# A planner's rule for PSUM banks at the attention visits, and a new order of all instructions

## The chip, the cores and the metric

The kernel runs on one core of a Trainium2 chip. The time is device microseconds of one execution; several runs give a median. The engines are PE (TensorE, matrix products), DVE (VectorE), ACT (ScalarE), POOL (GpSimd) and SP, whose queue issues nearly all DMAs.

## What is computed

The input is 64 graphs of 256 nodes with 512 features each, and one 256 x 256 adjacency that all of them share. Two attention layers follow each other, each with a layer norm and a ReLU in front and a residual behind. All is float32.

```python
h = jnp.maximum(_layernorm(x), 0.0)          # layer 0, one head, additive scores
Wh = h @ W
logits = (Wh @ a_src)[:, :, None] + (Wh @ a_dst)[:, None, :]
logits = jnp.where(logits >= 0, logits, 0.2 * logits)
attn = softmax(where(adj == 0, -inf, logits))
x = x + attn @ Wh

h = jnp.maximum(_layernorm(x), 0.0)          # layer 1, 8 heads of 64
q, k, v = split_heads(h @ Wq.T + bq), split_heads(h @ Wk.T + bk), split_heads(h @ Wv.T + bv)
attn = softmax(where(adj == 0, -inf, q @ k.T / 8))
x = x + (merge_heads(attn @ v)) @ Wo.T + bo
```

## The kernel before

**Graphs and pairs.** One graph is two tiles of 128 nodes. Graphs go in pairs, an even one g and an odd one g + 1, and 31 of the 32 pairs run the same stages. The names of the tiles tell the stages in the profile, since every instruction is issued from one line, 430.

**Stages of layer 0**, for each graph: `normalize0` (ACT computes mean and squares, then writes h), `weights0` (e1, e2 and em; their sums over the nodes go through PE as ps and prs; the row es_b is spread to all partitions by DMAs), `aggregate0` (PE products pu, which ACT copies into uT; POOL then forms the four sums us), and `transform0`, which multiplies by W and adds into x. In the profile that is po_a<-w_sb and po_b<-w_sb; in the programs' names po0.

**Stages of layer 1.** `normalize1` makes xn, and `transpose1` transposes it: DVE by blocks into z, then through DRAM (the DMAs rows and hT) into left. `project` makes q, k and v for a pair at once (the products pp, with weight sums that the DMAs wst bring in each time from `products` in DRAM). `attention` follows per graph, then `scale` and `output`, which multiplies by Wo (po_a<-wo_sb, po_b<-wo_sb; po1 in the programs' names) and stores.

**Products in series.** The projections and the two multiplications by W and Wo use Strassen's scheme with seven products instead of eight, the projections on two levels. `chained` runs seven products through two PSUM banks, a and b: a, b, a, b, a, b, a. After each product DVE (in some cases ACT) reads the bank and adds it into its target. Before the next product of the same bank may start, that read must be done. Such a series is a *chain*: it holds two banks from its first product to its last read. A block is what PE issues in one piece: four passes for po, six for pp.

**Attention and its visits.** `scores(e)` makes the scores of two heads, in two banks psc; four such steps (e = 0 to 3) fill eight banks, one after the other. ACT reads each bank with an exponential into ex. DVE multiplies ex by the mask (ex<-ex,pmask) and forms the sums sm. `values` makes pav from ex and v, which ACT copies into aT; `head_sums` makes psm, whose reciprocal rc goes by the DMAs row and rb to all partitions and scales aT. The planner joins the steps into three visits that PE runs in one piece: A is the scores of the even graph, B the values and head sums of the even graph with the scores of the odd one behind, C the values and head sums of the odd graph (`VISITS`, line 186).

**What sets the order.** All instructions are recorded first. `Plan.schedule` then simulates the engines with a cost for each instruction and writes an order for each of the five queues; on the chip every queue runs in that order, with semaphores. PE's blocks are sorted by a due place that `PHASE` gives to each stage (in units of graphs). At each point the planner takes the first block among the next `AHEAD` whose inputs are there and for which enough PSUM banks are open. Seven banks are shared out; the eighth keeps the mask. A block that opens a bank needs one, a block that opens a chain needs two, and the second one stays reserved (`reserved`) until the chain takes it. To enter a visit at least `ROOM` = 2 banks must be open besides the reserved ones; if they aren't, the planner goes on to later blocks. Inside a visit (`visit` is not empty) only its own blocks are taken. The engines' instructions are taken in the order of a latest time, which `SLACK` shifts. `SPARE`, `POOLED` and `LANDING` stretch the assumed times of DVE and ACT, of POOL and of DMAs.

The loop over PE's blocks is the place of the change:

```python
todo = [(blocks.index(visit[0]), visit[0])] if visit else enumerate(blocks[:ahead])
for n, block in todo:
    when = startable(block)
    ...
    if block.peers and not visit:
        need = max(need, ROOM)
    if len(open_banks) < need + others:
        continue
```

Of the kernel before, what the change touches and what calls it, by code (L numbers as in the profile page):

```python
# [144 lines left out]
class Op:  # L145
# [10 lines left out]


SIGNAL = 0.06
AHEAD = 24
SLACK = 4.95106  # L160
SPARE = 1.05024
STEPS = {"first": 6, "project": 49, "transform0": 7, "output": 7, "aggregate0": 3}
ASIDE = 0.9
PHASE = {
    "project0": [-0.11788, 0.21271, 0.48678, 1.00731, 1.0573, 1.46327, 1.80536, 2.01641],
    "aggregate00": [-1.17147, -0.98045],
    "aggregate01": [-0.53658, -0.25084],
    "output0": [2.37181, 2.56087, 2.64717],
    "output1": [3.26166, 3.33686, 3.61644],
    "transform00": [-1.01934, -0.99938, -0.77151],  # L170
    "transform01": [-0.48014, -0.39696, 0.06805],
    "weights00": [-1.85072],
    "weights01": [-0.68932],
    "A": [1.60905],
    "B": [2.0676],
    "C": [2.4008],
    "first0": [0.0443, 0.37448],
    "first1": [0.71863, 1.33943],
    "A0": [0.77194],
    "B0": [1.59602],  # L180
    "C0": [2.25334],
}
LANDING = 2.98188
POOLED = 1.1
ROOM = 2
VISITS = {(0, False): ("A", 0), (0, True): ("B", 0), (1, False): ("B", 10), (1, True): ("C", 0)}

# [1 line left out]
class Plan:  # L189
# [96 lines left out]
    def schedule(self, ahead, slack):  # L286
        self.deadlines(slack)
        left = {op.at: len(op.deps) for op in self.ops}
        ready = {e: [] for e in ("vector", "scalar", "gpsimd", "sync")}
        waiting = {e: [] for e in ready}  # L290
        free = dict.fromkeys((*ready, "tensor"), 0.0)
        times, now = [0.0], 0.0
        bank_free, reserved = [0.0] * (self.banks + 1), {}
        blocks, tile_kind, visit = list(self.blocks), None, []
        port = queue = 0.0

        def release(op):
            for o in op.next:
                left[o.at] -= 1
                if not left[o.at] and o.engine != "tensor":  # L300
                    known = max(ready_at(o, d) for d in o.deps.values())
                    heapq.heappush(waiting[o.engine], (known, o.at))
                    heapq.heappush(times, known)

        def ready_at(op, dep):
            if op.engine == dep.engine == "tensor":
                return dep.start + dep.step
            return dep.done + SIGNAL

        def finish(op, start):  # L310
            nonlocal port, queue
            spare = 1.0 if op.engine == "tensor" else POOLED if op.engine == "gpsimd" else SPARE
            op.start, op.done = start, start + op.time * spare
            end = start + op.step * spare
            if op.port:
                wait = max(0.0, port - start)
                op.done += wait
                port = max(port, start) + 0.05 if op.brief else op.done
                end += wait
            if op.transfer:  # L320
                queue = max(queue, start + 0.6 * LANDING) + op.transfer * SPARE
                op.done = queue + 0.4 * LANDING
            free[op.engine] = end
            heapq.heappush(times, end)
            release(op)
            for v in (*op.outs, *op.ins):
                base = v.base
                if base.bank is not None and all(o.done is not None for o in base.ops):
                    bank_free[base.bank] = max(o.done for o in base.ops) + SIGNAL
                    heapq.heappush(times, bank_free[base.bank])  # L330

        def startable(block):
            block = [op for b in block.peers for op in b] if block.peers and not visit else block
            inside = set(o.at for o in block)
            when = 0.0
            for op in block:
                for d in op.deps.values():
                    if d.at not in inside:
                        if d.done is None:
                            return None  # L340
                        when = max(when, ready_at(op, d))
            return when

        for op in self.ops:
            if not op.deps and op.engine != "tensor":
                heapq.heappush(waiting[op.engine], (0.0, op.at))
        total = len(self.ops)
        order = []
        while len(order) < total:
            assert times, [[o.outs[0].base.name for o in b][:1] for b in blocks[:4]]  # L350
            now = heapq.heappop(times)
            while times and times[0] <= now:
                heapq.heappop(times)
            for e in ready:
                while waiting[e] and waiting[e][0][0] <= now:
                    at = heapq.heappop(waiting[e])[1]
                    heapq.heappush(ready[e], (self.ops[at].late, at))
                if free[e] <= now and ready[e]:
                    op = self.ops[heapq.heappop(ready[e])[1]]
                    order.append(op)  # L360
                    finish(op, now)
            if free["tensor"] <= now:
                open_banks = [n for n, t in enumerate(bank_free[:-1]) if t <= now]
                todo = [(blocks.index(visit[0]), visit[0])] if visit else enumerate(blocks[:ahead])
                for n, block in todo:
                    when = startable(block)
                    if when is None or when > now:
                        if when is not None:
                            heapq.heappush(times, when)
                        continue  # L370
                    new = {
                        id(o.outs[0].base): o.outs[0].base
                        for o in block
                        if o.outs[0].base.bank is True
                    }
                    need, others = len(new), sum(reserved.values())
                    for base in new.values():
                        if base.chain is not None:
                            if base.chain in reserved:
                                others -= reserved[base.chain]  # L380
                            else:
                                need = 2
                    if block.peers and not visit:
                        need = max(need, ROOM)
                    if len(open_banks) < need + others:
                        continue
                    for base in new.values():
                        base.bank = min(open_banks, key=lambda b: bank_free[b])
                        open_banks.remove(base.bank)
                        bank_free[base.bank] = math.inf  # L390
                        if base.chain is not None:
                            reserved[base.chain] = reserved.get(base.chain, 2) - 1
                            if not reserved[base.chain]:
                                del reserved[base.chain]
                    t = now
                    late = now > free["tensor"] + 0.01
                    for op in block:
                        if op.kind != tile_kind:
                            t += 0.1 if tile_kind == (P, P) else 0.2
                            tile_kind, late = op.kind, True  # L400
                        finish(op, t)
                        t += op.step + (0.1 if late else 0.0)
                        late = False
                        order.append(op)
                    free["tensor"] = t
                    heapq.heappush(times, t)
                    del blocks[n]
                    if block.peers:
                        visit = (visit or block.peers)[1:]
                    break  # L410
        self.order = sorted(order, key=lambda op: ((op.block or [op])[0].start, op.at))
        return max(op.done for op in order)
# [97 lines left out]
def kernel(  # L510
# [1369 lines left out]
    with ExitStack() as ctx_b:  # L1880
# [5 lines left out]
        bounded(plan)  # L1886
        plan.schedule(AHEAD, SLACK)
        ps_mm = ctx_b.enter_context(tc.tile_pool(name="ps_mm", bufs=1, space=PSUM))
# [38 lines left out]
```

## Time and profile before

| | us |
|---|---|
| median of three runs | 2775.09 |
| lowest and highest | 2773.01, 2775.99 |
| the profiled execution | 2773.59 |
| its span, first to last instruction | 2771.7 |
| busy time of POOL, q1's share of the 16 DMA engines | 1195.3, 57.5% |
| ACT, exponentials ex<-psc, 512 of them | 259.8, mean 0.616 |
| DVE, masks ex<-ex,pmask, 512 of them | 317.0, mean 0.681 |
| DVE, sums sm<-ex, 256 of them | 167.4, mean 0.687 |
| wst<-products, 651 transfers of 384 KB, issue to landing | 4.6 |

A row of a group tells the engine, the operation, the tiles written and read, their shapes and the count; then the busy time in the whole run, the mean of one in nanoseconds, and the idle time before it with what ended that. A PE matmul's busy time reaches to its modelled end, some time after the next one has started, so a block's cost is read from its start to the start of the next block. A float32 product appears as two passes: 2048 rows of psc are 1024 matmuls.

In a timeline each row has the start, the length, the engine, the instruction and a count of neighbours that are merged.

### The profile page before, as it was taken

How to read it: one execution, taken by the hardware profiler on the slowest of the kernel's cores; microseconds unless marked ns; L12 is line 12 of the kernel's file. 1: busy time of each engine (PE TensorE's matmuls, PEld its weight loads, DVE VectorE, ACT ScalarE, POOL GpSimd, SP SyncE). 2: the span in 40 equal slices, each digit the busy share in tenths (PEclk: the TensorE clock that was granted, in tenths of full speed). 3: DMA queues.
4: the chain of work that ended last, by engine and by line, in shares of the span. 5: the costliest groups of instructions: out<-in, count | busy, mean ns of one | idle time of the engine just before them, and what ended most of it. 6: DMA issues, size and time to landing. Idle time of an engine off the chain costs nothing.

```text
span 2771.7 us, 60664 instructions
## 1 busy us (share of the span) xinstructions
PE 2733.5 (99%) x22588; PEld 2390.8 (86%) x22588; DVE 2224.5 (80%) x4879; ACT 1343.6 (48%) x3332; POOL 1195.3 (43%) x1153
## 2 busy tenths in 40 slices
PE   7999999999999999999999999999999999999998
PEld 5888888888888888888888888888898888888886
DVE  6677888888888888888788888888888888887876
ACT  5754454444554544544444545445545445444431
POOL 3344444444444444444444344444444444445431
PEclk9999999999999999999999999999999999999999
DMA  5455565565555655655655555565556656556662
GB/s 182 160 178 162 176 190 175 171 190 184 179 182 172 190 182 175 184 179 173 196 178 181 187 177 175 184 181 184 182 177 189 185 175 184 175 173 197 181 183 91
DMA packets 278926, 493.32 MB, mean 178 GB/s; under 512 B 45473, under 2 KB 150756, under 8 KB 278630
## 3 DMA queue, kind: packets, MB, share of 16 engines
q1 hardware_dynamic: 278534, 489.39, 57.5%
q8 instruction: 183, 3.00, 0.5%
q14 instruction: 113, 0.93, 0.1%
q0 software_dynamic: 96, 0.01, 0.0%
HBM read 405.09 MB, written 76.20 MB: 174 GB/s over the span
## 4 chain that ended last, share of the span: by engine, by line
PE 88%; DVE 3%; DMA 3%; ACT 3%; POOL 2%; issue 1%; SPq 0%; POOLq 0%; DVEq 0%
PE pp_a L430 20%; PE po_a L430 15%; PE pp_b L430 15%; PE po_b L430 11%; PE psc L430 9%; PE pu L430 8%; PE pav L430 4%; ACT xn L430 2%; PE psm L430 1%; DMA x<-in_x_dram 1%; POOL em L430 1%; PE pqk L430 1%; DMA out_dram<-x 1%; PE ps L430 1%; DVE nmr L430 1%; POOL rstd L430 1%
## 5 line engine op out<-in xcount | busy, mean ns | idle before, releaser
L430 POOL TENSOR_TENSOR c<-tt,c 128x768 f32<-128x768 f32 x124 | 232.6, 1896 | 402.8 <-DVE tt L430 305.8
L430 DVE TENSOR_TENSOR ex<-ex,pmask 128x512 f32<-128x512 f32 x512 | 317.0, 681 | 33.0 <-ACT ex L430 32.9
L430 PE MATMUL psc<-c 64*128 64x256 f32 x2048 | 292.1, 400 | 5.7 <-ACT aT L430 3.3
L430 DVE TENSOR_TENSOR x<-po_a,x 128x256 f32<-128x256 f32 x500 | 209.3, 419 | 107.9 <-PE po_a L430 105.3
L430 PEld LDWEIGHTS psc<-c 64*128 64x128 f32 x2048 | 205.6, 187 | 79.9 <-ACT ex L430 21.7
L430 ACT ACTIVATE ex<-psc 128x512 f32<-128x512 f32 x512 | 259.8, 616 | 28.9 <-PE psc L430 28.7
L430 POOL TENSOR_TENSOR us<-uT 128x256 f32<-128x256 f32 x126 | 107.8, 855 | 314.7 <-ACT uT L430 300.7
L430 PE MATMUL pu<-em,h 128*128 128x256 f32 x1008 | 239.0, 380 | 0.3 <-ACT c L430 0.3
L430 PE MATMUL pav<-ex,c 128*64 128x256 f32 x2048 | 235.1, 382 | 0.0
L430 ACT COPY uT<-pu 128x512 f32<-128x512 f32 x126 | 73.9, 586 | 322.4 <-PE pu L430 322.3
L430 DVE SCALAR_TENSOR_TENSOR junk<-wa,h 128x512 f32<-128x512 f32 x252 | 206.3, 819 | 21.9 <-ACT h L430 19.7
L430 PEld LDWEIGHTS pav<-ex,c 128*64 128x64 f32 x2048 | 141.4, 137 | 73.1 <-issue 0.9
L430 PEld LDWEIGHTS pu<-em,h 128*128 128x128 f32 x1008 | 184.9, 191 | 22.5 <-issue 0.7
L430 POOL TENSOR_TENSOR x<-x,bo_b 128x512 f32<-128x512 f32 x128 | 160.9, 1278 | 92.4 <-ACT xn L430 87.4
L430 ACT ACTIVATE e<-es_b,ed 128x256 f32<-128x256 f32 x122 | 61.1, 501 | 287.1 <-issue 158.0
L430 DVE TENSOR_TENSOR tt<-tt,pp_a 128x384 f32<-128x384 f32 x279 | 153.4, 550 | 50.9 <-PE pp_a L430 46.0
L430 POOL TENSOR_TENSOR as<-aT 128x256 f32<-128x256 f32 x62 | 67.3, 1085 | 286.4 <-DVE aT L430 277.9
L430 POOL TENSOR_TENSOR em<-e,maskT 128x512 f32<-128x512 f32 x62 | 78.9, 1273 | 257.4 <-DVE e L430 248.4
L430 DVE TENSOR_TENSOR c<-c,pp_a 128x384 f32<-128x384 f32 x217 | 119.2, 549 | 80.3 <-ACT xn L430 45.3
L430 DVE TENSOR_TENSOR x<-po_b,x 128x256 f32<-128x256 f32 x375 | 156.3, 417 | 31.2 <-PE po_b L430 27.4
L430 ACT ACTIVATE h<-x,nmr,rstd 128x512 f32<-128x512 f32 x128 | 100.4, 810 | 157.5 <-DVE nmr L430 153.3
L430 DVE TENSOR_TENSOR sm<-ex 128x512 f32<-128x512 f32 x256 | 167.4, 687 | 0.0
(274 smaller groups left out, 7510.6 us busy)
## 6 DMA issues: line engine op xcount, KB each, us to landing
wst<-products SPq DMA_DIRECT2D x651, 384.0 KB, 4.6
wst<-products SPq DMA_DIRECT2D x217, 192.0 KB, 4.4
x<-in_x_dram SPq DMA_DIRECT2D x64, 512.0 KB, 5.2
out_dram<-x SPq DMA_DIRECT2D x128, 256.0 KB, 2.3
rows<-z SPq DMA_DIRECT2D x62, 512.0 KB, 4.2
hT<-rows SPq DMA_DIRECT2D x248, 128.0 KB, 3.3
rb<-row SPq DMA_DIRECT2D x124, 256.0 KB, 4.2
products<-made SPq DMA_DIRECT2D x21, 384.0 KB, 2.8
```

Of the source, the lines that this page charges most:

```text
L430: getattr(getattr(self.nc, op.engine), op.method)(*map(real, op.args), **{k: real(a) for k, a in op.kwargs.items()})
```

## The change

In the planner's loop a flag is added. As soon as a visit has been met whose inputs are there, but which is not entered for lack of banks, no later block is taken that opens a bank, unless that bank is the second one of a chain which is already running. Blocks of running chains go on. The constants of the planner are new, and with them the order of all instructions and the numbers of the banks; the instructions themselves, the buffers and the DMAs stay as they are.

```diff
-AHEAD = 24
-SLACK = 4.95106
-SPARE = 1.05024
+AHEAD = 49
+SLACK = 8.77484
+SPARE = 1.01674
...
 PHASE = {
-    "project0": [-0.11788, 0.21271, 0.48678, 1.00731, 1.0573, 1.46327, 1.80536, 2.01641],
-    "aggregate00": [-1.17147, -0.98045],
-    "aggregate01": [-0.53658, -0.25084],
-    "output0": [2.37181, 2.56087, 2.64717],
-    "output1": [3.26166, 3.33686, 3.61644],
+    "project0": [-0.19438, 0.14752, 0.34467, 0.44171, 0.46305, 0.81839, 1.07542, 1.17863],
+    "aggregate00": [-1.53219, -1.41296],
+    "aggregate01": [-0.59454, -0.51794],
+    "output0": [2.23584, 2.29763, 2.36253],
+    "output1": [2.92165, 2.98377, 3.36758],
...
-    "A": [1.60905],
-    "B": [2.0676],
-    "C": [2.4008],
+    "A": [1.52703],
+    "B": [1.72599],
+    "C": [2.68772],
...
-LANDING = 2.98188
-POOLED = 1.1
+LANDING = 3.47999
+POOLED = 1.24146
...
                 todo = [(blocks.index(visit[0]), visit[0])] if visit else enumerate(blocks[:ahead])
+                draining = False
                 for n, block in todo:
...
                     if block.peers and not visit:
                         need = max(need, ROOM)
+                        draining = True
+                    elif draining and any(b.chain not in reserved for b in new.values()):
+                        continue
                     if len(open_banks) < need + others:
                         continue
```

Around the visits the order of one pair in the middle of the run changes thus. Before, A is followed by blocks of po1, po0 and pp in turn, and by B 24.0 us of PE work later (from scores to scores); after, A is followed by six blocks of po0, one pp, the seventh po0 and one more pp, and by B 15.7 us later. Before, the eight banks of A are 5, 7, 2, 3, 5, 7, 2, 3 and those of B's scores 5, 2, 4, 7, 3, 5, 2, 4; after, 2, 7, 0, 6, 1, 3, 5, 2 and 0, 7, 3, 5, 2, 0, 7, 3. On ACT the copy into aT stood between the writing of xn and the mean for the next h, with the exponentials of B behind all three; after, that copy stands ahead of xn, and the mean for h behind the exponentials.

More of the change, by code (lines that the diff above doesn't have):

```diff
@@ L164 @@
 PHASE = {
-    "project0": [-0.11788, 0.21271, 0.48678, 1.00731, 1.0573, 1.46327, 1.80536, 2.01641],
-    "aggregate00": [-1.17147, -0.98045],
-    "aggregate01": [-0.53658, -0.25084],
-    "output0": [2.37181, 2.56087, 2.64717],
-    "output1": [3.26166, 3.33686, 3.61644],
[L170 to L173, printed above, removed]
-    "A": [1.60905],
-    "B": [2.0676],
-    "C": [2.4008],
[L177 to L181, printed above, removed]
-}
-LANDING = 2.98188
-POOLED = 1.1
+    "project0": [-0.19438, 0.14752, 0.34467, 0.44171, 0.46305, 0.81839, 1.07542, 1.17863],
[3 more added lines that the diff above has]
+    "output1": [2.92165, 2.98377, 3.36758],
+    "transform00": [-1.77316, -1.33036, -1.07346],
+    "transform01": [-1.92842, -0.97066, -0.51583],
+    "weights00": [-1.72871],
+    "weights01": [-0.9223],
+    "A": [1.52703],
+    "B": [1.72599],
+    "C": [2.68772],
+    "first0": [0.80489, 0.83087],
+    "first1": [1.72404, 1.86629],
+    "A0": [0.70038],
+    "B0": [1.66422],
+    "C0": [2.86714],
+}
+LANDING = 3.47999
+POOLED = 1.24146
 ROOM = 2
```

## The prediction

> **What bounds the kernel now.** I read the page's first part, then the waits of PE, then its groups with shapes kept apart, then the timeline of one pair of graphs. The page says that PE is the bound and that its clock is granted in full.
>
> ```profile
> span 2771.7 us, 60664 instructions
> PE 2733.5 (99%) x22588; PEld 2390.8 (86%) x22588; DVE 2224.5 (80%) x4879; ACT 1343.6 (48%) x3332; POOL 1195.3 (43%) x1153
> PEclk9999999999999999999999999999999999999999
> ```
>
> 99% leaves 38 us of idle PE, and the list of its waits sums to 31 us, 25 of them in the first 300 us. So a gain has to come from inside the busy time. The groups show where:
>
> ```profile
> L430 PE MATMUL psc<-c 64*128 64x256 f32 x2048 | 292.1, 400 | 5.7 <-ACT aT L430 3.3
> ...
> L430 PE MATMUL pav<-ex,c 128*64 128x256 f32 x2048 | 235.1, 382 | 0.0
> ```
>
> psc (scores) and pav (values) have equal counts and 256 columns each, and both run two at a time on half of the array; the scores take 57 us more. The timeline shows it in every pair:
>
> ```profile
> 1386.89 4.41 PE L430 MATMUL psc<-c 64*128 64x256 f32 x32
> 1391.23 1.13 PE L430 MATMUL po_a<-wo_sb,aT 128*128 128x256 f32 x4
> ...
> 1411.68 4.85 PE L430 MATMUL psc<-c 64*128 64x256 f32 x32
> 1416.46 0.71 PE L430 MATMUL pp_a<-sa,wst 128*128 128x128 f32 x4
> ```
>
> From its start to the start of the next block, a visit to an even graph's scores takes 4.34 us, an odd graph's 4.78. Over the run 30 even visits take 4.34 and 28 odd ones 4.78. The next visit of the same kind begins 84.2 us later. Six visits are different, among them these:
>
> ```profile
> 126.04 3.72 PE L430 MATMUL psc<-c 64*128 64x256 f32 x32
> 129.69 1.13 PE L430 MATMUL pu<-em,h 128*128 128x256 f32 x4
> ...
> 202.01 3.92 PE L430 MATMUL psc<-c 64*128 64x256 f32 x32
> 205.86 0.71 PE L430 MATMUL pp_b<-sc,wst 128*128 128x128 f32 x4
> ```
>
> They take 3.65 and 3.85. The banks written into the programs explain them. A visit fills eight. Where the program gives it six or seven different ones (three visits) it takes 3.65. With five it takes 3.85 (202.01, and another at 2675.93) if ACT begins the exponentials at once. With four it takes 4.34: its fifth matmul waits for the first exponential. The odd ones have five banks as well, but take 4.78, because ACT comes late:
>
> ```profile
> 1411.28 1.52 ACT L430 ACTIVATE xn<-x,nmr,rstd 128x512 f32<-128x512 f32 x2 [1.52 <-DVE nmr L430]
> 1412.71 0.56 ACT L430 COPY aT<-pav 128x512 f32<-128x512 f32 x1
> 1413.17 0.63 ACT L430 ACTIVATE h<-x 128x512 f32<-128x512 f32 x1
> 1413.71 0.19 ACT L430 ACTIVATION_READ_ACCUMULATOR h<-x 128x1 f32 x1
> 1413.80 3.99 ACT L430 ACTIVATE ex<-psc 128x512 f32<-128x512 f32 x8
> ```
>
> In an even visit the first exponential starts 1.17 us after the visit (1388.06); here 2.12, so 0.95 late, and 3.85 + 0.95 is 4.80. Outside the visits PE runs from block to block: six passes of pp in 0.67, four of po in 0.865, with 0.1 at each change of tile shape.
>
> **The change, part by part.** PE's blocks are the same 3,435, DMAs and arithmetic are the same; shape changes go from 301 to 302, 0.1 us. What changes is order and banks, so I price the stalls that go and those that come, from the two programs' orders and the rows above. Distances below are PE work, counted in blocks at the spacings above.
>
> *Scores of even graphs.* All but one now have seven banks (the last six). 30 x (4.34 - 3.65) = 20.6 us gained. Ends: 20.6, and 0 if ACT were late there; the uT copy ahead of the exponentials stands there in both orders, so I take 20.6.
>
> *Scores of odd graphs.* Still five banks, since two stay with the product pp_0 that runs across the visit. But on ACT the aT copy now stands ahead of xn, and the mean for h behind the exponentials. That leaves the xn pair as the last hindrance. It waits for the layer norm of x, whose last addition comes about 0.3 us later against the values than now (next item). From 1407.04, where the values start, xn began at 4.24; it would begin at 4.54 and end at 6.06. The first exponential could start at 5.81, so it is 0.25 late: 4.10. 28 x (4.78 - 4.10) = 19.0 us gained; ends 0 (4.78) and 26.0 (3.85).
>
> *The third odd visit.* One visit, at 225.54, takes 10.57 us: ACT stood behind e, which waited for the es_b DMA. In the new order e follows the exponentials. I take 5 us of at most 6.7; the other end is 0.
>
> *The stretch after an even visit, the main cost.* Where PE had pp blocks between the products of po_a<-w_sb, it now runs six of these in a row, then a pp, then the seventh. Four times a bank is written again after only 0.865 us; before, the shortest turn in a steady pair is 1.09 inside a visit and 1.34 outside. Meanwhile DVE has the masks:
>
> ```profile
> 1388.68 4.28 DVE L430 TENSOR_TENSOR ex<-ex,pmask 128x512 f32<-128x512 f32 x7 [0.37 <-ACT ex L430]
> 1393.26 0.42 DVE L430 TENSOR_TENSOR x<-po_a,x 128x256 f32<-128x256 f32 x1 [0.30 <-PE po_a L430]
> 1393.60 0.68 DVE L430 TENSOR_TENSOR ex<-ex,pmask 128x512 f32<-128x512 f32 x1
> ```
>
> Masks follow each other at 0.60 ((4.28 - 0.68) / 6), and an addition holds DVE for 0.34. The new order puts one mask or sum between every two additions: 0.94 us a product against 0.865 on PE, 0.075 a product. A read starts 0.20 after its block (1393.06 to 1393.26) and lasts 0.42, so 0.2 of a turn is spare. Laid out from the first mask at 1.79 after the visit, only one turn comes too late, by 0.05; if each mask is just ahead of its read, the first two turns lose 0.4 each and the rest 0.075 apiece, some 1.0. Behind a turn that waits stands all of PE's queue, the values first. I take 0.2 a pair, nearer the lay-out: 30 x 0.2 = 6.0 us lost, ends 1.5 and 30. The same lay-out puts x's last addition 0.3 later. Next is the values visit, now 7.6 us after the scores instead of 15.8, and its head sums at 11.1 instead of 19.4. Eight masks, four sums and seven additions are 9.6 us from 1.79, so 11.4 after the visit's start; the head sums start at 14.7. Some 3.3 us cover it, and nothing is charged.
>
> A rule stands against that zero. Beside the first masks POOL works on us, and the row shows no harm: seven masks take 4.28 us in the even visit with three us instructions at their start, and 4.28 in the odd one, where POOL stops 0.3 us after the first. The Trainium skill ("SBUF — State Buffer", "Who interferes with whom") says that a VectorE instruction with two SBUF inputs and a GpSimd one that reads SBUF shut each other out for a whole instruction. By it four us instructions at their mean of 0.855 would put DVE 3.4 us back, past the cover by about 0.1 us a pair, and the sum would be 3 us higher; by the row it stays.
>
> *Other turns.* prs follows ps after 1.54 instead of at least 2.0 (even graphs), with two DVE instructions of 0.15 between, behind others of 0.5 to 0.6. The second pp_0 blocks come 0.37 us sooner after the odd visit, while ACT's copies, which ended 2.00 after it (1418.46), are wanted at 2.01. One turn of pp_3 is 1.04. The first addition of pp_6 stands on DVE behind a POOL addition of 1.9 us. Together 0 (turns of 1.34 cost nothing now) to 1.0 us a pair (each loses one DVE instruction of 0.5 in two of the four places); I take 0.4: 12 us lost.
>
> *DMAs.* The same transfers. The tightest turn of the six wst buffers goes from 5.1 to 5.8 us of PE work against 4.6 from issue to landing; es_b's from 2.0 to 6.4, rb's from 3.1 to 8.4, and hT's stays within 0.3. SP's other issues keep to the blocks that need them. Nothing is charged.
>
> *Head and tail.* Before the last pair's values PE keeps one pp block where it had twelve blocks, and the masks, then the sums, end some 0.5 us after their place: 1 us lost. The head's order moves by a few blocks: 0, with 5 either way.
>
> Sum: -20.6 - 19.0 - 5.0 + 6.0 + 12.0 + 1.0 = -25.6. The profiled execution took 2773.59 (its span 2771.7 and 1.9 around it), so 2748.0; the median of the runs is 1.5 above it: **2750**.
>
> **Rivals.** *All stalls go*, and no new one comes: odd visits at 3.85, all 6.7, no cost: 2775.1 - 53.3 = 2722. For it: today's plan has next to no wait outside the visits. Against: those four short turns. *ACT stays late*: the layer norm slips by another 0.7, the odd visits stay at 4.78 and the third visit with them: -20.6 + 19 = -1.6, so 2773. For it: ACT is wanted for 5.6 of 6 us around 1411; against: two instructions leave its path. *DVE sets the pace* after the even visit: if masks and additions cost their full 0.68 and 0.42, a product takes 1.10 and six lose 1.4 us a pair, 42 in all; xn then comes late too and the odd visits gain nothing: -20.6 - 5 + 42 + 13 = +29, so 2804. With the other gains kept it becomes slower from 1.04 us a product ((31.6 / 30) / 6 = 0.175 above 0.865). For it: DVE is already busy for 5.6 of 6 us after 1386.9; against: the spacing of 0.94. *The rule does nothing for the odd visits* is built in: banks stay at five.
>
> **How the numbers follow.** My sum 0.62, with its own range of 2736 to 2764; all stalls go 0.15; ACT late 0.12; DVE 0.11. Runs of this kernel spread by 0.1%, so I count 0.2%, 5.5 us, as told from no change: under 2769.5 faster, over 2780.6 slower. Faster: 0.60 of mine, 0.15, and 0.03 of ACT late, 0.78. Same: 0.02 + 0.08 = 0.10. Slower: 0.11 + 0.01 = 0.12. For the range I go down into the first rival and up past the second: 2731 to 2777.
>
> **What would show it.** Even visits 3.65 and odd ones near 4.1 from start to next block; the psc group at about 248 us instead of 292; a pair every 83.4 us. Waits of PE on DVE under po_a<-w_sb and po_b<-w_sb show the short turns; more than 1 us of them a pair makes me wrong, as does a first exponential over 1.6 us after an odd visit.

## The result, and the profile after

The changed kernel takes 2772.53 us, median of 12 runs (2768.96 to 2774.18); the kernel before, on the same chip, 2773.81 (2771.47 to 2775.99, 12 runs). The ratio is 0.9995 with a 95% interval of [0.9986, 1.0004]: no change that can be told. The forecast was 2750 and faster, and it is wrong, although the visits gained more than it said. All times below are against the kernel before on the same chip.

The page of the profile after, its head:

```profile
span 2770.4 us, 60428 instructions
...
PE 2706.9 (98%) x22588; PEld 2372.2 (86%) x22588; DVE 2278.4 (82%) x4879; ACT 1335.2 (48%) x3332; POOL 1205.5 (44%) x1153
```

PE is busy for 26.6 us less, in a span that is only 1.3 us shorter, so PE now waits. Its groups with shapes kept apart (busy, mean ns, idle time before):

```profile
L434 PE MATMUL psc<-c 64*128 64x256 f32 x2048 | 244.3, 385 | 0.0
...
L434 PE MATMUL pp_b<-sb,wst 128*128 128x128 f32 x496 | 78.5, 281 | 33.2 <-ACT c L434 33.2
```

The scores fell from 292.1 to 244.3 us. One group of the projections has a new wait: 33.2 us, all for ACT. (L430 of before is L434 here, and L442 in most of the experiments.) The timeline of one pair shows the visits, with DVE's additions between the masks:

```profile
1389.17 3.72 PE L434 MATMUL psc<-c 64*128 64x256 f32 x32
...
1392.82 1.13 PE L434 MATMUL po_a<-w_sb,uT 128*128 128x256 f32 x4
...
1393.99 0.42 DVE L434 TENSOR_TENSOR x<-po_a,x 128x256 f32<-128x256 f32 x1
1394.33 0.68 DVE L434 TENSOR_TENSOR ex<-ex,pmask 128x512 f32<-128x512 f32 x1
1394.93 0.42 DVE L434 TENSOR_TENSOR x<-po_b,x 128x256 f32<-128x256 f32 x1
...
1404.30 0.58 ACT L434 COPY aT<-pav 128x512 f32<-128x512 f32 x1 [1.09 <-PE pav L434]
1404.78 1.52 ACT L434 ACTIVATE xn<-x,nmr,rstd 128x512 f32<-128x512 f32 x2
...
1405.22 3.92 PE L434 MATMUL psc<-c 64*128 64x256 f32 x32
1406.38 4.03 ACT L434 ACTIVATE ex<-psc 128x512 f32<-128x512 f32 x8
...
1409.07 0.71 PE L434 MATMUL pp_a<-sa,wst 128*128 128x128 f32 x4
```

The even visit takes 3.65 from start to next block (1389.17 to 1392.82), the odd one 3.85 (1405.22 to 1409.07), and its first exponential begins 1.16 after it. Over the whole run 34 visits take 3.65 and 30 take 3.85; before, 30 took 4.34 and 28 took 4.78. All 64 together went from 293.3 to 239.7 us, so 53.6 were gained.

What was given back is found by taking PE's rows between 290 and 2650 us from start to start, and subtracting from each the usual spacing of its pass. What is left is the excess. Outside the visits it was 15.1 us and is now 69.6. Behind each wait the first passes of the next block lose about 0.10 us more; the table calls this the slow restart:

| place on PE, after | times | us each | sum with the slow restart behind it |
|---|---|---|---|
| pp_b<-sb after po_a (chain pp_4) | 27 | 1.347 | 39.1 |
| pp_a<-sd after po_b (chain pp_5) | 27 | 0.278 | 10.2 |
| the short turns of po0 after the even visit | 84 | 0.05 to 0.075 | 5.1 |

53.6 gained and 54.5 lost leave 0.9 more; the span is 1.3 shorter, so the ends, before 290 and behind 2650, gave 2.2. The first row is seen in this piece of the timeline (SPq is SP's queue of DMA issues):

```profile
1518.42 0.68 SPq L434 DMA_DIRECT2D es_b<-es_b  x1
...
1519.73 2.48 SPq L434 DMA_DIRECT2D out_dram<-x  x1
...
1526.62 1.03 PE L434 MATMUL po_a<-w_sb,us 128*128 128x256 f32 x4
1527.51 0.51 ACT L434 ACTIVATE e<-es_b,ed 128x256 f32<-128x256 f32 x1 [1.92 <-DMA es_b<-es_b]
1527.93 0.61 ACT L434 ACTIVATE c<-pp_b,bias 128x128 f32<-128x128 f32 x2
...
1528.43 0.26 ACT L434 COPY c<-pp_b 128x128 f32<-128x128 f32 x1
1528.74 0.71 PE L434 MATMUL pp_b<-sb,wst 128*128 128x128 f32 x4 [1.10 <-ACT c L434]
```

PE is through with po_a at 1527.49 and wants to write pp_b again. The bank is still to be read by ACT's three copies. They stand in ACT's queue behind the first e1 of an odd graph (the row e<-es_b,ed), and that one waits for the spread of es_b to 127 partitions, issued at 1518.42: e1 starts 9.1 us later, 0.1 us after the spread's semaphore. The waits of ACT say it too:

```profile
ACT e L434 <- DMA es_b<-es_b: 62.8, 31, 3.7
```

Before, ACT waited for the same transfer even longer, and in the middle of the run nothing stood behind it that PE wanted. The list of before names es_b for a part of it only, and has more under "issue", where the profile shows no releaser:

```profile
ACT e L430 <- issue: 158.3, 29, 7.2
...
ACT e L430 <- DMA es_b<-es_b: 66.5, 16, 5.4
```

By the semaphores of the trace, 60 of the 61 spreads of before end a wait of ACT: each time e1 starts less than 0.2 us after the spread has landed. These waits sum to 287.1 us. In the changed kernel 30 do, with 60.5 us. So the new order took most of this wait away, and put what was left of it ahead of copies that PE needs. The second row:

```profile
1547.69 3.60 POOL L434 TENSOR_TENSOR c<-tt,c 128x768 f32<-128x768 f32 x2
...
1550.12 1.20 DVE L434 TENSOR_SCALAR ve<-ssq 128x2 f32<-128x2 f32 x1
...
1550.68 1.03 PE L434 MATMUL po_b<-wo_sb,as 128*128 128x256 f32 x4
1551.23 0.54 DVE L434 TENSOR_TENSOR c<-tt,pp_a 128x384 f32<-128x384 f32 x1
...
1551.69 0.54 DVE L434 TENSOR_TENSOR c<-tt,pp_b 128x384 f32<-128x384 f32 x1
1551.83 0.71 PE L434 MATMUL pp_a<-sd,wst 128*128 128x128 f32 x4
```

ve has 128 x 2 elements, and takes 0.16 where POOL is idle. Here it takes 1.20 and ends at 1551.32, as POOL's instruction does at 1551.29. The additions out of pp_5 stand behind it, and PE, free at 1551.55, waits for the first.

### The profile page after: what moved, and what is told of

It is laid out like the page before. It is cut to its first block, busy times and chain, and to the rows that moved or that the text cites. A ratio compares the mean times of both kernels' runs of the same rounds, so it can differ in the third digit from the quotient of the medians.

```text
span 2770.4 us, 60428 instructions
## 1 busy us (share of the span) xinstructions
PE 2706.9 (98%) x22588; PEld 2372.2 (86%) x22588; DVE 2278.4 (82%) x4879; ACT 1335.2 (48%) x3332; POOL 1205.5 (44%) x1153
## 4 chain that ended last, share of the span: by engine, by line
PE 82%; DMA 10%; DVE 5%; ACT 1%; issue 1%; SPq 0%; ACTq 0%; DVEq 0%
PE pp_a L434 17%; PE po_a L434 13%; PE pp_b L434 12%; PE po_b L434 10%; DMA es_b<-es_b 9%; PE psc L434 9%; PE pav L434 8%; PE pu L434 6%; PE psm L434 2%; DVE c L434 2%; DVE ve L434 1%; PE pqk L434 1%; ACT c L434 1%; PE ps L434 1%; PE po L434 1%
## 5 line engine op out<-in xcount | busy, mean ns | idle before, releaser
L434 DVE TENSOR_TENSOR ex<-ex,pmask 128x512 f32<-128x512 f32 x512 | 319.4, 681 | 38.0 <-ACT ex L434 38.0
L434 POOL TENSOR_TENSOR rstd<-ve,minus_half 128x2 f32<-128x2 f32 x128 | 89.9, 703 | 444.9 <-DVE ve L434 439.3
L434 DVE TENSOR_TENSOR x<-po_a,x 128x256 f32<-128x256 f32 x500 | 209.2, 419 | 88.4 <-PE po_a L434 87.0
L434 ACT ACTIVATE ex<-psc 128x512 f32<-128x512 f32 x512 | 257.7, 628 | 38.6 <-PE psc L434 36.3
L434 ACT ACTIVATE h<-x,nmr,rstd 128x512 f32<-128x512 f32 x128 | 100.4, 810 | 363.6 <-DVE nmr L434 363.5
L434 POOL TENSOR_TENSOR c<-tt,c 128x768 f32<-128x768 f32 x124 | 238.5, 1944 | 19.1 <-DVE c L434 8.5
L434 POOL TENSOR_TENSOR us<-uT 128x256 f32<-128x256 f32 x126 | 106.2, 843 | 321.9 <-ACT uT L434 319.3
L434 PE MATMUL psc<-c 64*128 64x256 f32 x2048 | 244.3, 385 | 0.0
L434 PE MATMUL pav<-ex,c 128*64 128x256 f32 x2048 | 235.2, 382 | 0.0
L434 PE MATMUL pu<-em,h 128*128 128x256 f32 x1008 | 234.7, 382 | 0.0
L434 PEld LDWEIGHTS psc<-c 64*128 64x128 f32 x2048 | 201.3, 187 | 30.9 <-issue 10.7
L434 DVE SCALAR_TENSOR_TENSOR junk<-wa,h 128x512 f32<-128x512 f32 x252 | 210.4, 835 | 15.0 <-ACT h L434 9.1
L434 DVE TENSOR_TENSOR tt<-tt,pp_a 128x384 f32<-128x384 f32 x279 | 154.0, 552 | 74.8 <-PE pp_a L434 72.1
L434 ACT ACTIVATE xn<-x 128x512 f32<-128x512 f32 x126 | 79.4, 630 | 277.5 <-DVE x L434 277.4
L434 POOL TENSOR_TENSOR x<-x,bo_b 128x512 f32<-128x512 f32 x128 | 160.9, 1278 | 118.5 <-ACT xn L434 118.5
L434 PEld LDWEIGHTS pu<-em,h 128*128 128x128 f32 x1008 | 188.4, 192 | 23.3
L434 PEld LDWEIGHTS pav<-ex,c 128*64 128x64 f32 x2048 | 141.4, 137 | 73.4 <-issue 1.4
L434 POOL TENSOR_TENSOR em<-e,maskT 128x512 f32<-128x512 f32 x62 | 79.1, 1276 | 275.9 <-DMA wst<-products 202.5
L434 ACT ACTIVATE c<-pp_a,bias 128x128 f32<-128x128 f32 x186 | 58.1, 363 | 253.8 <-PE pp_a L434 253.8
L434 DVE TENSOR_TENSOR c<-c,pp_a 128x384 f32<-128x384 f32 x217 | 119.4, 550 | 74.0 <-ACT c L434 51.6
L434 DVE TENSOR_TENSOR x<-po_b,x 128x256 f32<-128x256 f32 x375 | 157.1, 419 | 26.8 <-PE po_b L434 21.6
L434 DVE TENSOR_TENSOR c<-c,pp_b 128x384 f32<-128x384 f32 x279 | 153.3, 549 | 27.8 <-ACT c L434 23.1
```

The source lines that it names most:

```text
L434: getattr(getattr(self.nc, op.engine), op.method)(*map(real, op.args), **{k: real(a) for k, a in op.kwargs.items()})
```

## The experiments

| kernel | us, median | ratio to before, 95% |
|---|---|---|
| e_es: changed kernel, first e1 of odd graphs moved | 2750.16 | 0.9923 [0.9908, 0.9938] |
| e_nowait: changed kernel, that e1 without its wait | 2746.78 | 0.9916 [0.9901, 0.9931] |
| e_ve: changed kernel, ve moved | 2759.41 | 0.9963 [0.9949, 0.9977] |
| e_banks: changed kernel, even visits with four banks | 2792.30 | 1.0073 [1.0058, 1.0089] |
| e_rule: before with the draining rule alone | 2773.55 | 1.0003 [0.9993, 1.0012] |
| e_both: e_es and e_ve together | 2735.63 | 0.9867 [0.9851, 0.9884] |
| e_out: e_both, one store moved on SP | 2721.88 | 0.9819 [0.9803, 0.9836] |
| e_act: e_both, the spread of es_b issued by ACT | 2723.32 | 0.9823 [0.9807, 0.9840] |

Before was 2771.36 beside the first four (9 runs) and 2772.97 beside the last four (13 runs). The moves are made in the finished order of the planner, with a helper, `put_behind`, that puts one instruction behind others on the same engine. The code below shows the lines that differ, without this helper.

**Is it the first e1 of the odd graph on ACT?**

```diff
+for g in range(5, 64, 2):
+    plan.put_behind(
+        lambda op: op.engine == "scalar" and op.outs[0].base.name == f"e1_{g}",
+        lambda op: op.engine == "scalar" and op.ins[0].base.name == f"pp_{g - 3}_4_b",
+    )
```

> The changed order, with one instruction moved in 28 pairs: the first e1 of the odd graph, which reads es_b, goes behind ACT's copies out of pp_4_b. My theory: in the changed order this e1 stands ahead of those copies and waits for the es_b DMA (9.1 us from issue to landing at 1518.42), so PE waits 1.35 us at pp_b<-sb and loses 0.10 more in restarting, 39 us in 27 pairs. Then the time falls from 2772.5 to about 2733 (2728 to 2742), the pair from 84.6 to 83.2, and the gap ahead of pp_b<-sb is under 0.1. Rival one, the copies are late by ACT's or DVE's own work: over 0.8 us of the gap stays, time 2762 to 2773. Rival two, something else sets the pair anyway (DVE at 82%, or the chain from e through em, ps and prs to pu): the gap goes but PE waits elsewhere as much, time above 2755.

It took 2750.16, outside the 2728 to 2742 of the theory. The wait ahead of pp_b<-sb is gone from PE's list, so the mechanism holds, but the gain was some 22 us and not 39, since rival two came true in part. A new wait stands ahead of the very next block, pp_a<-S: 27 times 0.531, 14.3 us by starts. The profile's own list counts only what lies behind the modelled end of the block before:

```profile
PE pp_a L442 <- DMA wst<-products: 7.0, 17, 0.6
```

-39.1 + 14.3 and 1.9 for its restarts is -22.9 (the medians differ by 22.4, and by the ratios to before it is 20). The next late thing was a transfer of wst.

**Is it the wait, or the place and the half microsecond of e1?** The instruction stays where it is and reads the mask, which is always there.

```diff
+masks = next(op for op in plan.order if op.outs and op.outs[0].base.name == "maskT").outs[0]
+for g in range(5, 64, 2):
+    op = next(op for op in plan.order if op.outs and op.outs[0].base.name == f"e1_{g}")
+    op.args = (op.args[0], masks[:, 0, :], *op.args[2:])
```

> The changed order with nothing moved; the same e1 instruction reads the mask in place of es_b, so that it has no DMA to wait for (half of e1 of the odd graphs is then formed from the mask). It still takes its 0.5 us of ACT at the same place. My theory, it is the wait for es_b and not the place in the queue that costs: about 2733 as in the run with the move, within 5 us of it, and the gap ahead of pp_b<-sb under 0.2. If the 0.5 us of ACT between the copies is what costs: 0.5 to 0.9 of the 1.35 us stays, 2750 to 2760. If neither: 2765 to 2773.

2746.78: the forecast of 2733 fails as it did above, because the wait for wst is there again (27 times 0.495). But as much is gained with e1 left ahead of the copies, so what cost the time is the wait for es_b and not the place of e1.

**Is it ve that makes the second row?**

```diff
+for g in range(6, 64, 2):
+    reads = [op for op in plan.order if op.engine == "vector" and op.ins[-1].base.name == f"pp_{g - 4}_5_b"]
+    plan.put_behind(
+        lambda op: op.engine == "vector" and op.outs[0].base.name == f"ve0_{g}",
+        lambda op: op in reads[1:2],
+    )
```

> The changed order with one DVE instruction moved in 29 pairs: ve of the next even graph goes behind the second pair of additions out of pp_5. My theory: ve (1.20 us at 1550.12, while POOL runs the additions c<-tt,c until 1551.29) holds DVE, the additions come late and PE waits 0.28 us and 0.10 in restarting ahead of pp_a<-sd, 10 us in all. Then the time is 2772.5 - 10 = 2762 (2759 to 2766) and ve ends no later than now. Rival, DVE is simply full there: the gap stays above 0.2, time 2770 to 2775.

2759.41, and the excess ahead of pp_a<-sd is gone. The wait for ACT stays in this run, so the two are separate:

```profile
PE pp_b L442 <- ACT c L442: 31.8, 28, 1.9
```

At its new place the moved ve no longer meets POOL. Of the 112 ve from 290 us on, 28 others still do, at the very end of POOL's instruction, and take 0.23.

**Are the even visits' 0.69 us the banks?** Steps 3 and 4 of 29 even graphs get the banks of steps 1 and 2.

```diff
+banks = {op.outs[0].base.name: op.outs[0].base for op in plan.order if op.engine == "tensor"}
+for g in range(4, 62, 2):
+    for e in (2, 3):
+        for r in range(2):
+            banks[f"psc_{g}_{e}_{r}"].bank = banks[f"psc_{g}_{e - 2}_{r}"].bank
```

> The changed order; only the bank numbers of the scores of 29 even graphs are others: the third and fourth step use the banks of the first and second, four banks as before the change. My theory, the number of banks decides the visit: it takes 4.34 us again in place of 3.65, 29 x 0.69 = 20 us, time 2792 (2788 to 2797). Rival, ACT's place in the visit decides: it stays under 3.9, time 2771 to 2778.

2792.30. The timeline has the even visit back at its old length, and the odd one untouched:

```profile
1397.17 4.41 PE L434 MATMUL psc<-c 64*128 64x256 f32 x32
...
1401.51 1.13 PE L434 MATMUL po_a<-w_sb,uT 128*128 128x256 f32 x4
```

1401.51 - 1397.17 is 4.34, and 29 visits take that; the 30 odd ones stay at 3.85. Four banks against seven are worth 0.69 us a visit, and this gain reaches the end of the kernel in full: 29 x 0.69 is 20.0; the medians differ by 19.8, and by the ratios to before it is 22.

**Does the rule do it?**

```diff
+draining = False
 for n, block in todo:
...
     if block.peers and not visit:
         need = max(need, ROOM)
+        draining = True
+    elif draining and any(b.chain not in reserved for b in new.values()):
+        continue
```

> The kernel before with the draining rule alone, and none of the new constants. Theory: the rule never acts, every queue keeps its order and every semaphore its value, and the ratio to before is 1.000 within 0.001; all visits stay at 4.34 and 4.78. Rival: the rule is what spreads the scores over more banks; then even visits fall to 3.65 and it is some 20 us faster.

2773.55, ratio 1.0003. The program is the same as before, instruction for instruction, and so is the changed kernel's when the rule is taken out of it. Its group of scores:

```profile
L434 PE MATMUL psc<-c 64*128 64x256 f32 x2048 | 291.2, 399 | 5.8 <-ACT aT L434 3.4
```

So the rule acts nowhere, under the old constants or the new ones. All that this change does comes from the new constants.

**Do the two moves add up?**

> The changed kernel with both moves at once: on ACT the first e1 of each odd graph behind the copies out of pp_4_b, and on DVE ve behind the additions out of pp_5_b. If the two waits are separate, this takes what the second move alone took (10.2 us ahead of pp_a<-sd) off the first one's 2750: 2740, between 2735 and 2746; the new wait ahead of pp_a<-S stays at 27 x 0.53. If the second wait is only another place for the same lateness, it stays at 2748 to 2752 and the 10 us turn up at pp_a<-S or behind.

2735.63, within the range for two separate waits; the excess ahead of pp_a<-S is 13.2 us.

**Why is wst late then?** The timeline of e_es at that place:

```profile
1505.25 0.68 SPq L442 DMA_DIRECT2D es_b<-es_b  x1
1506.56 2.42 SPq L442 DMA_DIRECT2D out_dram<-x  x1
...
1509.05 4.25 SPq L442 DMA_DIRECT2D wst<-products  x4
...
1515.34 0.68 PE L442 MATMUL pp_a<-S,wst 128*128 128x128 f32 x4 [0.20 <-DMA wst<-products]
```

The store of x takes 2.42 us to be issued; most stores take 0.34. Only behind it comes the transfer that PE is waiting for, into a buffer that had been free since 1507.7. Either the store is slow, or SP is held by the spread of es_b ahead of it.

```diff
+for g in range(5, 64, 2):
+    queue = [op for op in plan.order if op.engine == "sync"]
+    spread = [n for n, op in enumerate(queue) if op.outs and op.outs[0].base.name == f"es_b_{g}"][-1]
+    if spread + 1 < len(queue) and not queue[spread + 1].outs:
+        store = queue[spread + 1]
+        plan.put_behind(
+            lambda op: op is store,
+            lambda op: op.engine == "sync" and op.outs and op.outs[0].base.name == f"wst_{g - 3}_4_5",
+        )
```

> Both moves, and on SP the store out_dram<-x that stands behind the spread es_b<-es_b goes behind the transfer of wst_4_5 (28 pairs). In the first experiment this store's issue took 2.42 us instead of 0.34, and wst_4_5, whose buffer was free 1.3 us earlier, was issued behind it and came 0.53 us late. Theory A: the store itself is slow there; then wst_4_5 is issued at once in 0.33, the wait ahead of pp_a<-S goes, and 27 x 0.53 + 2 = 16 us are gained on the kernel with both moves: about 2724. Theory B: SP is held by the spread of es_b to 127 partitions, and whatever is issued next is slow; then the store takes 0.34, the issue of wst_4_5 takes 1.2 or more, and it still ends some 0.5 us sooner than now: 0 to 16 us gained, most of the wait gone, 2724 to 2740.

2721.88. The queue in e_out:

```profile
1491.91 0.68 SPq L442 DMA_DIRECT2D es_b<-es_b  x1
1494.56 1.43 SPq L442 DMA_DIRECT2D wst<-products  x1
1496.04 0.75 SPq L442 DMA_DIRECT2D out_dram<-x  x1
```

Now it is the transfer of wst whose issue is long, 1.43 us where the median of all is 0.32. In both kernels, e_es and e_out, what stands next is through some 3.9 us after the spread began (28 odd graphs each, medians 3.90 and 3.91, from 3.4 to 4.2). So theory B. But the issue of wst starts 2.65 us behind the spread's start and not 3.80, and the wait ahead of pp_a<-S is gone.

```diff
+for g in range(5, 64, 2):
+    spread = [op for op in plan.order if op.engine == "sync" and op.outs and op.outs[0].base.name == f"es_b_{g}"][-1]
+    spread.engine = "scalar"
```

> Both moves, and the spread es_b<-es_b of the odd graphs is issued by ACT instead of SP (28 pairs). Theory B (SP is held by that spread): the store out_dram<-x takes 0.34 on SP again, wst_4_5 is issued 1.3 us sooner, the wait ahead of pp_a<-S goes: 2724, between 2720 and 2732, as ACT is idle there. Theory A (the store itself is slow): the store keeps its 2.4 us and the wait stays: 2740. A third way: ACT waits for the row of es_b ahead of its copy into uT, po0 comes late, and it is slower than with both moves alone, by up to 0.5 us a pair (2754).

2723.32, and in the trace of e_act (ACTq is ACT's queue of DMA issues):

```profile
1494.15 0.34 SPq L442 DMA_DIRECT2D out_dram<-x  x1
1494.23 0.62 ACTq L442 DMA_DIRECT2D es_b<-es_b  x1
...
1495.48 0.32 SPq L442 DMA_DIRECT2D wst<-products  x1
```

1.25 us behind the spread SP issues its transfer in 0.32, in each of the 28 pairs. Issued by ACT, the spread doesn't hold SP. ACT's copy into uT had begun ahead of it (1494.15), so the third way did not come.

The best kernel is e_out, 1.8% faster than before. Its head:

```profile
span 2719.9 us, 60373 instructions
...
PE 2694.1 (99%) x22588; PEld 2377.1 (87%) x22588; DVE 2265.6 (83%) x4879; ACT 1340.0 (49%) x3332; POOL 1208.6 (44%) x1153
```

The excess outside the visits is 21.5 us there, against 69.6 in the changed kernel and 15.1 before; the visits take 239.7 us as in the changed kernel.

## Why the prediction was wrong

In sum, -25.6 was forecast and -1.3 came. The visits gave 53.6 where 44.6 was forecast, but a wait that the sum had put at nothing took 39.1 of it. A pair in the middle of the run takes 84.60 us and not the 83.4 of the forecast; it took 84.22 before, and only the ends of the run, with the third odd visit, make up for that.

**The visits**: right, and low in two of three terms. Even visits: 20.6 forecast, 30 x 0.69 measured, and e_banks confirms the cause. Odd visits: 19.0 forecast, but they take 3.85 and not 4.10, so 28 x 0.93 = 26.0, the upper end that was given. The term took the last addition into x to come 0.3 later and hold xn back; in the trace x is complete at 1400.60 and xn waits for the copy into aT alone: it begins 4.20 after the values (1400.58 to 1404.78) and not 4.54. The third odd visit gave all of its 6.7 instead of 5.0.

**The stretch after an even visit**: right. 6.0 forecast, 5.1 measured. DVE's additions follow each other 0.94 us apart (1393.99, 1394.93), as laid out.

**The rule set against that zero** spoke of other instructions than these. The mask pmask lies in a PSUM bank, so ex<-ex,pmask has one SBUF input, and the Trainium skill ("SBUF — State Buffer", "Who interferes with whom") names two. The trace after agrees: from 290 us on, masks take 0.68 in the median whether POOL is at work as they start (143) or not (337), while aT<-aT,rb, which reads two tiles in SBUF, takes 1.12 (58 times) instead of 0.68 (58).

**Other turns**: 12.0 forecast for ps, pp_0, pp_3 and pp_6. In the blocks of those places PE lost at most 3.5 us, so this term was too large. A turn that was not named, at pp_5, lost 10.2 by ve, which the prediction doesn't mention. Before's own trace could have told it: there 57 of the 112 ve from 290 us on start while POOL is at work, and take up to 1.30.

**DMAs, "Nothing is charged"**: this is the step that failed, and it is worth 39 us: ACT's e1 waited for the spread of es_b in the new order too, PE waited 1.35 us a pair behind it, and both waits went when e1 read the mask instead (e_nowait). The step set the turn of wst against 4.6 us from issue to landing, and es_b's new distance of 6.4 us of PE work against nothing. The list of transfers shows no landing for the spread, but the chain of waits of before had it twice, and its timeline shows it in a steady pair:

```profile
140.71 8.15 DMA es_b<-es_b
...
213.94 8.69 DMA es_b<-es_b
...
1391.43 0.69 SPq L430 DMA_DIRECT2D es_b<-es_b  x1
...
1398.68 0.51 ACT L430 ACTIVATE e<-es_b,ed 128x256 f32<-128x256 f32 x1 [5.50 <-issue]
```

From the issue to e1 are 7.25 us here, and 6.4 is less than that and than 8.15. But the distance alone doesn't tell the cost: it was 2.0 before, and ACT waited longer, for nothing that PE wanted. What the new order changed is the instructions behind the one that waits. The prediction asked what is queued behind a waiting instruction for PE's queue after the even visit. Asked of ACT's queue here, the question leads to the copies out of pp_4 and to PE. The third odd visit of the old order (10.57 us, ACT behind e) had shown just this wait, and the prediction used it as a gain and did not ask where else e would stand.

**The next wait behind it** sits in the same step: wst was called the tightest turn and left uncharged. Its transfers keep their distance; what delays one of them is SP, held by the spread. It stays hidden behind the wait for ACT until that is gone.

**The rivals.** "All stalls go", 2722, had 0.15. It is not what the change does, but it is where its order arrives once three instructions a pair are moved: e_out's 2721.88. "ACT stays late" came near the time (2773) by another way: its mechanism, odd visits at 4.78, did not occur. That the rule does nothing was allowed for the odd visits only; it does nothing at all.

**Head and tail**: 1.0 lost was forecast. Before 290 us and behind 2650 the changed kernel gained 2.2, beside what its visits gained there.

What stays open: why the spread holds its queue. The DMA packets in the traces tell when. A spread is 127 packets of 1 KB that start one after another, 0.042 us apart, 5.4 us in all, in before (56 spreads, 290 to 2650 us) and for the odd graphs of the changed kernel alike. The first packet starts 1.3 us after the issue in before and 3.1 us after it for those odd graphs. What is next in SP's queue is through about 1 us later, at 2.4 (27 stores) and at 3.9 us. So both the late landing and the long hold go with a late first packet. No run shows what makes the first packet late, or why the next issue has to wait for it.

## What to carry to other kernels

Before calling a new order free, take every instruction on the in-order engines that waits for a transfer, set its distance against that transfer's own measured landing (a spread of one row to 127 partitions is not like a large block), and ask what stands behind it: here the old order waited longer for the same transfer and lost nothing by it. A gain in the visible stalls is worth what the next late thing leaves of it: here a wait of 14 us lay hidden behind one of 39, with one of 10 beside them, and each went with one instruction's place. When a rule and new constants come together, run each alone.

## What the runs showed of the hardware

- The spread es_b<-es_b (127 rows of 1 KB) landed 7.2 us after its issue in before (median of 56, 290 to 2650 us) and 9.0 us after it in the changed kernel (odd graphs), where a wst transfer of 384 KB takes 4.6 and 4.9. A DMA right behind it on the same queue is through only 2.4 us (before, stores) or 3.9 us (changed order; a store or a transfer of wst) after the spread's start. With the spread on ACT's queue, SP's next DMA isn't held (0.32 us, 1.25 us later).
- A DVE instruction of 128 x 2 elements can last until the end of POOL's. In the trace after, 55 of the 112 ve from 290 us on start while POOL is at work, and every one of these ends 0.023 to 0.029 us after POOL's instruction (0.22 to 1.20 us long); the other 57 take 0.158 to 0.171. The Trainium skill ("SBUF — State Buffer", "Who interferes with whom") says that such a tensor_scalar can take the port pair shared with GpSimd, and that who comes second is blocked for the whole instruction: the rows agree.
- A visit takes 3.65, 3.85 or 4.34 us with seven, five or four PSUM banks, if ACT begins about 1.17 us after it (1.16 and 1.17 in the rows shown).
